# Two stacked graph attention layers: finishing work of the first entry spread over steps, the held row tile taken whole, first queries moved ahead

## The chip, the core and the metric

The kernel runs on one core of one Trainium2 chip. The metric is the device time in microseconds. Three runs of the kernel before gave 4408.67, 4412.6 and 4412.98, median 4412.6.

## The reference

`x` has 8 entries (batch) of 2048 rows and 256 columns; `adj` is a 2048 x 2048 integer mask. Cut to what matters:

```python
# layer 0: 8 heads of 32 columns
x_proj = einsum('bnd,hdf->bhnf', x, W)
e = leaky_relu(e_src[..., :, None] + e_dst[..., None, :], 0.2)
e = e + softplus(beta) * log(adj + 1e-6)          # where adj > 0
h = einsum('bhij,bhjf->bhif', softmax(e), x_proj)
x = layernorm(x + h.reshape(B, N, D) @ W_out.T)
# layer 1: one head
e = leaky_relu((x @ W1) @ (x @ W2).T, 0.2)        # where adj > 0
x = layernorm(x + relu(softmax(e) @ (x @ W3)))
```

## The kernel before

**Layer 0** (`class Gat`, one object per entry). The softmax over a row splits into products: the numerator for key row j and query row i is the larger of two factors times the mask, so that no exponential of a full matrix is needed. `step` does one unit of it: one of four head pairs (`hp`) and one of 16 tiles of key rows (`jt`), 64 units per entry. For each of the two heads VectorE makes `s` (L375) from the query factors `c`, a per-row scalar of `re`, and the mask tile `mt`. TensorE then multiplies `s` with the scaled values `v` into `val` and with `re` into `den`, the denominators (L410, both by `products`). For some units of later entries (`SUMMED`) the denominators are first added up by VectorE into `d` (L386), and TensorE sums `d` once at the end of the head pair.

When a head pair is done, `finish` copies `val` to `ht` and `den` to `dn`, turns the denominators into reciprocals (`rc`, L431), writes them to `rec_d` in DRAM, and, on every second head pair, loads them back spread over partitions (`rb`, L446) and multiplies each half of `ht` with them (L452). It is a generator: each `yield` is a place where it can be left and taken up later. Entries from 1 on put it into the list `later`, from which every `step` takes it one piece further; entry 0 runs it to its end at once (L401 to L403). For entry 0 `rb` lies in the two buffers of the tag `d`, which also take every second mask tile when `deep` is set (L201).

`factors` and `scale` prepare an entry: maxima and exponentials of the row scores (L280 to L288), and four multiplications of `v` (L294), each of four row tiles. `store` writes `v` and `re` to DRAM, and `load` brings `v` back in four pieces.

**Layer 1** (`class Dot`, one object per entry). `queries` makes `h1` for four row tiles (L530), `scores` the scores `e` of one row tile against all 2048 rows (L540) and their exponentials `p`, and `step` transposes `p` (`pt`, L563, copied to `pts`) and multiplies it with the values `h3` into `acc` (L579). It keeps one row tile ahead: while tile it is multiplied, the scores of it + 1 are made. `fill(0)`, `fill(1)` and `fill(2)` are places within `step` where units of the next entry's layer 0 are put. `output` (L479 to L492) makes `y`, adds the input tile `xg` and normalises it, four row tiles at a time; `turn` transposes it to `x1t` (L504) and makes `h3` (L510), eight pieces and a start.

**Order.** First layer 0 of entry 0 runs, and beside it the projections of the other seven entries (`others`, L270) and the weights. Then the loop at L669 interleaves layer 1 of entry b - 1 with layer 0 of entry b. TensorE's instructions are issued in the order of the program throughout (L88), those of the load queue on SyncE from L667 on. All other engines get an order from the scheduler when the kernel is built, and each engine then runs its own list in that order. Tiles of one tag share its buffers: a new tile waits until the last reader of an older one is done.

At each change of entry the last two row tiles of layer 1 are held back, and the first units of the next entry are put between their parts: tile 14 takes two units in `fill(1)` and two in `fill(2)`, tile 15 two in `fill(1)` together with the first piece of `output` (L694 to L699). Then come four groups of `output` with `turn` two groups behind, two units after each (L701 to L708), and then the new `Dot` with its queries and first scores.

Of the kernel before, what the change touches and what calls it, by code (L numbers as in the profile page):

```python
# [27 lines left out]
def kernel(  # L28
# [28 lines left out]
    H, _, DH = w_proj.shape  # L57
    NT = N // P
# [175 lines left out]
    class Gat:  # L234


        def __init__(self, b):
            self.b = b
            self.units = ((hp, jt) for hp in range(NP) for jt in range(NT))
            self.ms, self.mts = [], []  # L240
            self.later = gats[b - 1].later if b > 1 else []

        def begin(self, kept):

# [103 lines left out]
        def step(self, count=1):  # L348

            for _ in range(count):  # L350
                hp, jt = next(self.units)
                for work in list(self.later):
                    if next(work, self) is self:
                        self.later.remove(work)
                if self.b > 0 and hp == NP - 1 and jt == 0 and self.b + 1 < B:
                    gats[self.b + 1].load_factors()
                if jt == 0:
                    if self.b > 0:
                        self.cs = [self.cs_ahead.pop(0) for _ in range(HP)]
                    else:  # L360
                        self.cs = [self.query_rows(hp * HP + a) for a in range(HP)]
                    self.val = pacc.tile([P, HALF], F32, tag="val", name="val")
                    self.den = pacc.tile([P, HALF], F32, tag="den", name="den")
                first = self.b == 0 and hp == 0
                if first:
                    self.more_mt(jt + 2, jt > 0)
                if self.b > 0:
                    mt = self.mts.pop(0)
                else:
                    mt = self.mts[jt] if first else load_mt(jt, True)  # L370
                s = []
                for a in range(HP):
                    h = hp * HP + a
                    sa = wide_tile("s", "s", 4)
                    nc.vector.scalar_tensor_tensor(sa, self.cs[a], self.re[:, 0, jt, h:h + 1], mt, ALU.max, ALU.mult)  # L375
                    s.append(sa)
                    if self.b > 0 and jt == NT - 1:
                        self.cs_ahead += [c for c in [next(self.c_loads, None)] if c]
                if self.b > 0 and len(self.mts) < (4 if not SUMMED[self.b][hp] and jt < NT - 4 else 2):
                    self.mts += [t for t in [next(self.mt_loads, None)] if t]  # L380
                v, e = self.v, self.re[:, 1]
                heads = [hp * HP + a for a in range(HP)]
                chain = SUMMED[self.b][hp]
                if jt - 1 in chain[1:]:
                    for d, sa, h in zip(self.sums, self.last, heads):
                        nc.vector.scalar_tensor_tensor(d, sa, e[:, jt - 1, h:h + 1], d, ALU.mult, ALU.add)  # L386
                self.last = s
                self.products(self.val, [v[:, jt, ts(h, DH)] for h in heads], s, jt == 0, jt == NT - 1)
                if jt in chain[:1]:
                    self.sums = [wide_tile("d", "d", 2) for _ in heads]  # L390
                    for d, sa, h in zip(self.sums, s, heads):
                        nc.scalar.activation(d, sa, AF.Copy, scale=e[:, jt, h:h + 1])  # L392
                if jt not in chain:
                    self.products(self.den, [e[:, jt, h:h + 1].to_broadcast([P, DH]) for h in heads], s, jt == 0,
                                  not chain and jt == NT - 1)
                if chain and jt == NT - 1:
                    self.products(self.den, [ones] * HP, self.sums, False, True)
                if jt == NT - 1:
                    work = self.finish(hp)
                    next(work)  # L400
                    if self.b == 0:  # L401
                        for _ in work:
                            pass  # L403
                    else:
                        self.later.append(work)

        def products(self, dst, weights, s, start, stop):
            for c in range(HALF // BK):
# [46 lines left out]
        def output(self):  # L455


            b = self.b
            xb = x[b].rearrange("(t p) d -> p t d", p=P)
            xs = []  # L460

            def load(g):
                xs.append(chunk.tile([P, IG, D], F32, tag="ht", name="xg", bufs=3))
                nc.sync.dma_start(xs[g], xb[:, ts(g, IG), :])

            load(0)
            load(1)
            yield
            for g in range(NB):
                if 0 < g < NB - 1:  # L470
                    load(g + 1)
                st = small.tile([P, IG, nc.vector.BN_STATS_DIM], F32, name="st4", bufs=1)
                mv = small.tile([P, IG, nc.vector.BN_AGGR_DIM], F32, name="mv4", bufs=2)
                z = self.ht[:, ts(g, IG)].rearrange("p t k i -> p t (k i)")
                for k in range(0, IG, 2):
                    y = mm_tile("y").rearrange("p (t c) -> p t c", t=2)
                    for i in range(2):
                        for kc in range(KC):
                            nc.tensor.matmul(y[:, i, :], self.ht[:, g * IG + k + i, kc, :], wot[:, kc, :],  # L479
                                             start=(kc == 0), stop=(kc == KC - 1))  # L480
                    nc.vector.tensor_add(z[:, k:k + 2, :], y, xs[g][:, k:k + 2, :])
                    for i in range(k, k + 2):
                        nc.vector.bn_stats(st[:, i, :], z[:, i, :])
                        nc.vector.bn_aggr(mv[:, i, :], st[:, i, :])
                f = small.tile([P, 2, IG], F32, name="f4", bufs=2)
                nc.scalar.activation(f[:, 0, :], mv[:, :, 1], AF.Ln, bias=eps_ln)
                nc.scalar.activation(f[:, 0, :], f[:, 0, :], AF.Exp, scale=-0.5)
                nc.vector.scalar_tensor_tensor(f[:, 1, :], mv[:, :, 0], -1.0, f[:, 0, :], ALU.mult, ALU.mult)
                for k in range(IG):
                    nc.scalar.activation(z[:, k, :], z[:, k, :], AF.Identity, bias=f[:, 1, k:k + 1],  # L490
                                         scale=f[:, 0, k:k + 1])
                nc.scalar.dma_start(x1_d[b].rearrange("(t p) d -> p t d", p=P)[:, ts(g, IG), :], z)  # L492
                yield
# [22 lines left out]
    class Dot:  # L516


        def __init__(self, gat):
            self.b, self.x1t, self.h3 = gat.b, gat.x1t, gat.h3  # L520
            self.at = 0
            self.queries(0)
            self.scores(0)

        def queries(self, g):
            self.h1 = h1 = chunk.tile([P, KC, BK], F32, tag="ht", name="h1", bufs=3)
# [82 lines left out]
    def others():  # L609
# [1 line left out]

        order = gats[2:-2] + gats[1:2] + gats[-2:]
        groups = [(gat, g) for gat in order for g in range(NB)]
        xgs, xts = [], []

        def load(n):
            if n < len(groups):
# [11 lines left out]
        for n, (gat, g) in enumerate(groups):  # L629
            if g == 0:  # L630
                if gat is order[-1]:

                    for _ in range(IG):
                        yield
                gat.begin("h3" if n // NB % 2 or gat is order[-1] else "v")
            for k in range(IG):
                gat.row(g * IG + k, xts[n])
                if k == 1:
                    turn(n + 1)
                if g == NB - 1 and k == IG - 1:  # L640
                    gat.factors()
                    for i in range(NB):
                        gat.scale(i)
                    if gat.b > 1:
                        gat.store()
                if g == 0 and k == IG - 1 and n > 0:
                    groups[n - 1][0].queries()
                yield
        order[-1].queries()
        yield  # L650

# [17 lines left out]
    for b in range(1, B + 1):  # L669
# [11 lines left out]
        rows, turns = gat.output(), gat.turn()  # L681
        if dot is None:
            layer_0(4)
            next(rows)
            next(projections)
        else:

            dot.step(lambda k: layer_0((0, 2, 2)[k]))
            if not fresh:
                for work in gat.later:  # L690
                    for _ in work:
                        pass

            def fill(k):  # L694
                if k == 1:
                    layer_0(2)
                    next(rows)

            dot.step(fill)  # L699

        for g in range(NB + 2):  # L701
            if g < NB:
                next(rows)
            if g > 1:
                next(turns)
                next(turns)
            if g < NB + 1:
                layer_0(2)  # L708
        dot = Dot(gat)
        dot.step(lambda k: layer_0((2, 0, 2)[k]))  # L710
        count = NP * NT - (18 if b == 1 else 20)
        for i in range(NT - 3):
            n = (i + 1) * count // (NT - 3) - i * count // (NT - 3)
            dot.step(lambda k: layer_0((0, n - 2, 2)[k]))
# [31 lines left out]
```

## Time and profile before

| what | us | share |
|---|---|---|
| span of the profiled run | 4410.4 | |
| TensorE, matmuls | 4248.7 | 96% |
| VectorE | 3603.8 | 82% |
| ScalarE | 1663.4 | 38% |

By stage (busy time within a window, in us):

| window | what runs | TensorE | VectorE | DMA share |
|---|---|---|---|---|
| 0 to 160 | set-up, first head pair of entry 0 | 127.5 | 124.9 | 0.86 |
| 160 to 520 | rest of entry 0, projections | 326.1 | 291.7 | 0.73 |
| 596 to 1115 | layer 1 of entry 0, layer 0 of entry 1 | 499.1 | 436.8 | 0.62 |
| 1115 to 1626 | the same, one entry on | 499.8 | 449.9 | 0.53 |
| 4091 to 4410 | layer 1 of the last entry alone | 305.2 | 71.6 | 0.15 |

A row of the timeline has the start, the busy time, the engine, the line, the operation, the tiles, and in brackets the idle time before it and who ended that. A row of the waits has the engine and line that waited, what it waited for, the total in us, how often, and the longest. A row of the windows has, for each engine in turn, busy time and count, then the granted TensorE clock as a share of full speed, the DMA share and GB/s.

### The profile page before, as it was taken

Reading aid. Unit: us, or ns where it says so; the run is one execution under the profiler, and the core shown is the slowest. Engines: PE = TensorE matmul, PEld = TensorE weight load, DVE = VectorE, ACT = ScalarE, POOL = GpSimd, SP = SyncE. Lnnn points to the kernel's source line nnn. Section 1 sums busy time; section 2 is a strip of 40 time slices with the busy share of each in tenths; the row PEclk is TensorE's granted clock in tenths of the full one; section 3 lists DMA queues with packets and bytes.
Section 4 is the critical chain, followed back from the end, with each engine's and each line's share of the span. In section 5 each row is a group of like instructions: output and inputs, shape, how many; then the busy total and the mean of one; then the engine's idle time right before and its main releaser. Section 6 shows DMA issues by size and latency. Waiting matters only on the chain.

```text
span 4410.4 us, 59810 instructions
## 1 busy us (share of the span) xinstructions
PE 4248.7 (96%) x25072; PEld 2215.7 (50%) x25072; DVE 3603.8 (82%) x2606; ACT 1663.4 (38%) x3019; POOL 9.5 (0%) x14
## 2 busy tenths in 40 slices
PE   7989899998999999999999999999999999999999
PEld 4444354444555545554455544554455545555666
DVE  7878878898799988999789988999799997998222
ACT  7522143332333333433343333333333324333455
POOL 0000000000000000000000000000000000000000
PEclk9999999999999999999999999999999999999999
DMA  8867755656455564546555464555544465543211
GB/s 260 303 247 256 259 194 211 229 199 227 174 186 191 202 216 147 193 182 212 194 181 196 158 234 167 193 191 207 194 172 172 183 229 185 184 174 143 78 48 41
DMA packets 253166, 839.10 MB, mean 190 GB/s; under 512 B 32224, under 2 KB 150752, under 8 KB 178400
## 3 DMA queue, kind: packets, MB, share of 16 engines
q1 hardware_dynamic: 217568, 801.71, 51.2%
q10 hardware_dynamic: 35328, 33.56, 2.2%
q8 instruction: 196, 3.21, 0.3%
q14 instruction: 74, 0.61, 0.0%
HBM read 761.53 MB, written 73.14 MB: 189 GB/s over the span
## 4 chain that ended last, share of the span: by engine, by line
PE 50%; DVE 21%; issue 7%; DMA 7%; ACT 3%; SPq 1%; DVEq 0%; ACTq 0%
DVE s L375 14%; PE e L540 13%; PE acc L579 12%; PE val L410 10%; PE den L410 7%; DMA mt<-mt_d 4%; PE pt L563 3%; DVE d L386 3%; DMA rb<-rec_d 2%; PE h3p L510 2%; PE h1p L530 1%; PE y L479 1%; DVE p L545 1%; ACT d L392 1%; ACT p L548 1%
## 5 line engine op out<-in xcount | busy, mean ns | idle before, releaser
L375 DVE SCALAR_TENSOR_TENSOR s<-c,re,mt 128x2048 f32<-128x2048 f32 x1024 | 2354.2, 2342 | 218.6 <-PE den L410 141.0
L410 PE MATMUL val<-s,v 128*32 128x512 f32 x8192 | 1044.3, 605 | 90.7 <-DVE s L375 90.5
L579 PE MATMUL acc<-h,pts 128*128 128x256 f32 x4096 | 953.8, 380 | 12.1 <-ACT pts L565 12.1
L540 PE MATMUL e<-x1t,h 128*128 128x512 f32 x2048 | 905.2, 594 | 8.0 <-ACT h L532 8.0
L579 PEld LDWEIGHTS acc<-h,pts 128*128 128x128 f32 x4096 | 747.5, 190 | 107.4 <-ACT pts L565 22.1
L410 PE MATMUL den<-s,re 128*32 128x512 f32 x5648 | 706.1, 594 | 0.0
L386 DVE SCALAR_TENSOR_TENSOR d<-s,re,d 128x2048 f32<-128x2048 f32 x264 | 615.3, 2345 | 0.0
L540 PEld LDWEIGHTS e<-x1t,h 128*128 128x128 f32 x2048 | 379.4, 190 | 460.3 <-issue 415.8
L410 PEld LDWEIGHTS val<-s,v 128*32 128x32 f32 x8192 | 245.1, 110 | 723.0 <-issue 510.5
L565 ACT COPY pts<-pt 128x512 f32<-128x512 f32 x512 | 297.1, 583 | 762.6 <-PE pt L563 747.5
L545 DVE CUSTOM_DVE_ANT_0 p<-p,pen 128x2048 f32<-128x2048 f32 x128 | 292.7, 2286 | 243.8 <-ACT p L542 243.4
L542 ACT ACTIVATE p<-e 128x512 f32<-128x512 f32 x512 | 304.3, 595 | 466.3 <-PE e L540 459.5
L410 PEld LDWEIGHTS den<-s,re 128*32 128x32 f32 x5648 | 192.7, 110 | 426.0 <-issue 420.0
L563 PEld LDWEIGHTS pt<-ident,p 128*128 128x128 f32 x2048 | 239.0, 141 | 228.8 <-issue 182.7
L548 ACT ACTIVATE p<-p,neg 128x2048 f32<-128x2048 f32 x128 | 256.8, 2006 | 218.1 <-DVE neg L545 218.1
L563 PE MATMUL pt<-ident,p 128*128 128x128 f32 x2048 | 319.9, 279 | 5.1 <-ACT p L548 5.1
L585 DVE TENSOR_TENSOR z<-z,x1r 128x256 f32<-128x256 f32 x128 | 54.0, 422 | 182.7 <-ACT z L584 181.3
L584 ACT ACTIVATE z<-acc,rec 128x256 f32<-128x256 f32 x128 | 60.8, 475 | 373.3 <-PE acc L579 289.9
L510 PE MATMUL h3p<-w3s,x1t 128*128 128x256 f32 x512 | 124.7, 388 | 13.5 <-ACT x1t L505 13.0
L270 PE MATMUL proj<-wp,xt 128*128 128x272 f32 (+1 forms) x512 | 130.9, 401 | 3.2 <-ACT v L272 1.8
L272 ACT COPY v<-proj 128x256 f32<-128x256 f32 x128 | 47.0, 376 | 211.4 <-PE proj L270 197.5
L479 PE MATMUL y<-wot,ht 128*128 128x256 f32 x512 | 117.6, 383 | 0.0
(89 smaller groups left out, 1926.0 us busy)
## 6 DMA issues: line engine op xcount, KB each, us to landing
mt<-mt_d SPq DMA_DIRECT2D x496, 1024.0 KB
c<-c_d SPq DMA_DIRECT2D x64, 1024.0 KB
pen<-pen_d SPq DMA_DIRECT2D x112, 512.0 KB
xg<-in_x_dram SPq DMA_DIRECT2D x60, 512.0 KB
adj_t<-in_adj_dram SPq DMA_DIRECT2D x16, 1024.0 KB
mt_d<-mt SPq DMA_DIRECT2D x16, 1024.0 KB
rb<-rec_d SPq DMA_DIRECT2D x128, 128.0 KB
x_d<-ht ACTq DMA_DIRECT2D x32, 512.0 KB
```

The lines of the kernel that those rows point to most:

```text
L375: nc.vector.scalar_tensor_tensor(sa, self.cs[a], self.re[:, 0, jt, h:h + 1], mt, ALU.max, ALU.mult)
L386: nc.vector.scalar_tensor_tensor(d, sa, e[:, jt - 1, h:h + 1], d, ALU.mult, ALU.add)
L410: nc.tensor.matmul(dst[ts(q, DH), ts(c, BK)], weights[q % 2], s[q % 2][:, ds(q // 2 * HALF + c * BK, BK)], start=start, stop=stop)
L479: nc.tensor.matmul(y[:, i, :], self.ht[:, g * IG + k + i, kc, :], wot[:, kc, :], start=(kc == 0), stop=(kc == KC - 1))
L510: nc.tensor.matmul(t[:, ts(i, D)], x1t[:, kc, ts(2 * (j - 1) + i, P)], w3s[:, kc, :], start=(kc == 0), stop=(kc == KC - 1))
L540: nc.tensor.matmul(t, self.h1[:, kc, ts(it % IG, P)], self.x1t[:, kc, ts(c, BK)], start=(kc == 0), stop=(kc == KC - 1))
L542: nc.scalar.activation(p[:, ts(c, BK)], t, AF.Prelu, alpha=ALPHA)
L545: nc.vector.tensor_tensor_reduce(p, p, pen, -1.0, FMAX, ALU.add, ALU.min, neg)
L548: nc.scalar.activation(p, p, AF.Exp, bias=neg, scale=-1.0, accum_out=den)
L563: nc.tensor.transpose(t[:, ts(k, P)], p[:, ts(g * IG + k, P)], ident)
L565: nc.scalar.copy(pt, t)
L579: nc.tensor.matmul(acc, now[:, ts(k, P)], self.h3[:, j, :], start=(j == 0), stop=(j == NT - 1))
```

## The change

It has four parts. Entry 0's `finish` is no longer run to its end at once but put into `later` as for the other entries; the last one is carried on by entry 1's steps. The scalings of an entry's `v` and its `store` are spread over the next row tiles of the projections rather than done in a row. The last held row tile of layer 1 (15) is done in one piece, with two units of the next entry before it (in tile 14's `fill(2)`) and two behind it. And the new `Dot` makes its first queries before the last piece of `turn`, which makes the last values `h3`; its first scores come behind as before. `output` loads one input tile ahead from the start rather than two at once. The first entry takes 20 units ahead of layer 1's main loop, as the others do, rather than 18. The purpose is to keep TensorE supplied at these joints.

```diff
@@ class Gat
-            self.later = gats[b - 1].later if b > 1 else []
+            self.later = gats[b - 1].later if b > 0 else []
...
                     work = self.finish(hp)
                     next(work)
-                    if self.b == 0:
-                        for _ in work:
-                            pass
-                    else:
-                        self.later.append(work)
+                    self.later.append(work)
@@ output
             load(0)
-            load(1)
             yield
             for g in range(NB):
-                if 0 < g < NB - 1:
+                if g < NB - 1:
                     load(g + 1)
@@ Dot.__init__
             self.queries(0)
-            self.scores(0)
@@ others
                 if g == NB - 1 and k == IG - 1:
                     gat.factors()
-                    for i in range(NB):
-                        gat.scale(i)
+                    gat.scale(0)
+                    later = [lambda gat=gat, i=i: gat.scale(i) for i in range(1, NB)]
                     if gat.b > 1:
-                        gat.store()
+                        later.append(gat.store)
@@ main loop
             layer_0(4)
+            next(projections)
             next(rows)
-            next(projections)
         else:
             dot.step(lambda k: layer_0((0, 2, 2)[k]))
...
-            def fill(k):
-                if k == 1:
-                    layer_0(2)
-                    next(rows)
-
-            dot.step(fill)
+            next(rows)
+            dot.step()
+        layer_0(2)
 
         for g in range(NB + 2):
             if g < NB:
                 next(rows)
             if g > 1:
                 next(turns)
+                if g == NB + 1:
+                    dot = Dot(gat)
                 next(turns)
             if g < NB + 1:
                 layer_0(2)
-        dot = Dot(gat)
+        dot.scores(0)
         dot.step(lambda k: layer_0((2, 0, 2)[k]))
-        count = NP * NT - (18 if b == 1 else 20)
+        count = NP * NT - 20
```

In `others` one entry of the list `later` is taken after each row tile.

## The prediction

> **What bounds the kernel now.** I read the busy shares and the costliest groups first, then busy time by stage, then TensorE's gaps in the timeline, then what VectorE waits for at those gaps.
>
> ```profile
> PE 4248.7 (96%) x25072; PEld 2215.7 (50%) x25072; DVE 3603.8 (82%) x2606; ACT 1663.4 (38%) x3019; POOL 9.5 (0%) x14
> ...
> L375 DVE SCALAR_TENSOR_TENSOR s<-c,re,mt 128x2048 f32<-128x2048 f32 x1024 | 2354.2, 2342 | 218.6 <-PE den L410 141.0
> ```
>
> TensorE is the wall: 161.7 of 4410.4 us are not busy, so all that a reordering can win lies in there. VectorE mostly waits for TensorE (141.0 us before L375). The windows of the middle entries confirm it (1115 to 1626 us: TensorE 499.8 of 511). The gaps sit at the joints:
>
> ```profile
> DVE ht L452 <- DMA rb<-rec_d: 7.0, 1, 7.0
> DVE s L375 <- DMA mt<-mt_d: 3.7, 1, 3.7
> ...
> 303.32 1.92 PE L410 MATMUL val<-s,v 128*32 128x512 f32 x2 [11.07 <-DVE s L375]
> 507.97 1.92 PE L410 MATMUL val<-s,v 128*32 128x512 f32 x2 [12.15 <-DVE s L375]
> ...
> 1556.52 1.92 PE L410 MATMUL val<-s,v 128*32 128x512 f32 x2 [3.75 <-DVE s L375]
> 1580.33 1.06 PE L410 MATMUL val<-s,v 128*32 128x512 f32 x8 [1.68 <-DVE s L375]
> 1644.31 1.99 PE L510 MATMUL h3p<-w3s,x1t 128*128 128x256 f32 x8 [1.34 <-ACT x1t L505]
> 1650.63 0.70 PE L540 MATMUL e<-x1t,h 128*128 128x512 f32 x1 [0.90 <-ACT h L532]
> ...
> 304.00:310.00 6.00, 5.65 (x26) 1.09 (x27) 6.00 (x3) 0.00 (x0) 0.00 (x0) 0.53 0.98 397
> 1540.00:1606.00 66.00, 59.09 (x362) 30.98 (x364) 59.55 (x61) 14.96 (x35) 0.00 (x0) 0.95 0.63 209
> ```
>
> The bracket is TensorE's idle time before the row and who ended it. The two waits of VectorE (280 to 312 us) are those behind the 11.07: entry 0's division waits for its denominators, and the next mask tile could only load after it. In the windows the columns are TensorE, weight load, VectorE, ScalarE, GpSimd, clock: after a long gap the clock is 0.53 for 6 us, and in 1540 to 1606 both engines have nearly the same busy time (59.1 and 59.6 of 66).
>
> **The skill.** "TensorE: Matmul & The Clock Gate", Part 1, says the array falls to half clock after some 3.4 us idle. The trace agrees: 0.53 above, and 0.50 in 1556 to 1562 after the 3.75. So a gap of 4 us or more costs some 3 us on top (6 us at half speed), unless VectorE is late anyway. "Perfetto Trace Analysis", Identifying the Most-Contended Engine, warns that TensorE's busy share overstates it, while VectorE's occupancy is fair; hence I price joints by VectorE's list of work. "DMA: Bandwidth & Descriptors", Bandwidth, gives 435 GB/s as the ceiling; windows here show up to 423 (508 to 514 us).
>
> **The parts.** A unit is one `step` of layer 0: two L375 (2 x 2.3 = 4.6 us) on VectorE, `val` and `den` on TensorE (1.7 us each net, 3.65 with the tail). Units are counted from 0 at each head pair. The changed program's instruction order, as built, tells what stands behind what.
>
> 1. *Entry 0, second head pair done (gap at 303).* The division no longer blocks: unit 1's L375 follow at once (they end near 291.8 instead of 305.5), units 2 and 3 end near 296.8 and 302.1 (unit 3's tile takes the slot of unit 1's and is asked for at 291.8; loads here land in 4.8 to 6 us). TensorE finishes unit 3 at 306.0 instead of 321.1, about 11.07 plus the clock's 3 and a little waiting. But a wait comes instead: the order now has the factors (L280) and four L294 of a later entry *before* unit 5, where the kernel before had them after it. L280 waits for that entry's last projection, which TensorE reaches at 309.8 (unit 3 + 4.8 of projections, as from 321.1 to 325.9): 310.5 + 2.1 (L280 to L294, as at 326.85 to 328.97) + 4.6 + second multiply 1.2 + 4.6 = 323.0 for unit 5, while TensorE ended unit 4 at 314.4. New gap 8.6. Then projections, unit 6: it ends at 333.6 (336 with a cold clock) instead of 341.3. Taken: **-7** (bounds -2 and -14).
>
> 2. *Entry 0 to 1 (gap at 508).* VectorE idles for 3.78 (mask tile) plus some 5 us from 490 on. Spread out it does unit 1 at 490.0 to 494.6, factors and one L294 to 498.2, units 2, 3 to 507.4, three L294 to 510.9, unit 4 to 515.5, unit 5 with the first multiply to 521.3, unit 6 525.9, unit 7 530.5, layer norm of the first group with second multiply to 536.2, unit 8 540.8, unit 9 (adds of the next group between its halves, 3.2) 548.6. A unit takes VectorE 4.6 and TensorE 3.65, so TensorE starves: 3.3 + 4.4 + 2.1 + 1.1 + 4.1 = 15.0 us idle, against 12.15 + 1.22 + 0.55 and some 2.5 of half clock = 16.4 before. The `y` work that filled it now comes two units later. Behind the mask tile that waits for the first multiply stand `v_d`, `c_d`, the second pair of `rb` loads and unit 8's tile: 5 MB at about 423 GB/s is 12 us from 519, landing near 531, in time for 536. Taken: **-1** (bounds -7 and +5).
>
> 3. *Held row tile undivided (six joints, entries 1 to 6 to their followers).* TensorE does `acc` before units 4 and 5, filling the gap of 3.75. But VectorE's list from unit 4 (1546.19) to unit 7 is the same: four L375 pairs 18.4, four L386 9.4, two multiplies 2.4, row tile and first group some 4: about 34, and it runs with 0.8 us idle. Unit 7 is ready near 1580.2 in both (before: 1580.28). The gap moves behind `y`: TensorE is free at 1564.8 and gets unit 6 at 1572.3. Unit 9 ends near 1596 in both, perhaps a little later by the clock. Taken: 5 x +0.5; at the first such joint, where the mask tiles come late (a wait of 3.97 before unit 4), +2 by the same sum. Together 4.5, taken as **+4** (bounds +12 and -39, rival B).
>
> 4. *First queries ahead of the last values.* `h1p` (3.60 us) needs only the first 512 columns of `x1t`, ready long before. It fills the wait for the last `x1t` copy, and the last `h3p` (1.9) hides the copies of `h1`. Gaps removed at six joints: 1.33 or 1.34 each, 8.0 in all, and before `e` 1.05, 0.90, 0.76, 0.57 and 0.72 at five of them, 4.0 in all. Taken **-12**; the last joint has no such gap (`h3p` runs on into `h1p` there). The wait for a third PSUM buffer is hidden: each tile's copy is done one group earlier.
>
> 5. *Scaling spread, and one prefetch of `xg`.* In most places the order still has four L294 in a row, so the 4.18 gap at 444 stays. Near 144 one L294 falls behind unit 6's pair: **-1**. The `xg` loads cost nothing: they come earlier or at the same place, ahead of mask tiles that land before use. Entry 1 starts layer 1 two units further: same work, shared 44 to 13 instead of 46; 0, within 3.
>
> Sum: -7 - 1 + 4 - 12 - 1 = -17, 4412.6 to **4396**.
>
> **The rivals.**
> A, the two long gaps of entry 0 vanish whole: -14 and -15.5 instead of -7 and -1, 4374. For it: VectorE is only 291.7 of 360 us busy from 160 to 520 and could catch up. Against: the order of L280 above.
> B, the held tile wins its gap: 3.75 + 0.35 + some 3 of clock at six joints is 41 beside my 4: about 4351. For it: the wait is in the trace. Against: VectorE's full list until unit 7.
> C, waits take the place of those removed: the slots that `rb` shares with the mask tiles starve VectorE (part 1 at 0, part 2 at +8), and each held tile loses 2.5 as TensorE idles 7.5 us and comes back at half clock (+15): 0 + 8 + 15 - 12 = +11, about 4424, slower.
>
> **Numbers.** My forecast 0.68, spread about 8 us either way from parts 1, 2, 3; A 0.12, B 0.08, C 0.12. Within 0.2% means 4403.8 to 4421.4. About a sixth of the forecast's weight lies above 4403.8, so faster is 0.76, same 0.14, slower 0.10. The range leaves out B and most of C: 4372 to 4413.
>
> **What would show it.** Right: no gap at 303, a new one of 8 to 9 us some 15 to 20 us later before a `val`, ended by L375; smaller gaps adding to about 15 between 495 and 550; in each later joint no gap before `acc` but 4 to 8 us behind the first `y` group; none before the last `h3p`. Wrong: steps of later entries shorter than 508 us (B), or VectorE waiting for `mt` or `rb` for over 5 us after the first multiply (C).

## The result, and the profile after

The changed kernel takes 4390.02 us (median of 4 runs, 4388.77 to 4394.88) beside 4412.79 for the kernel before on the same chip: ratio 0.9952, 95% interval 0.9935 to 0.9970. That is about 21 us less (13 to 29 by the interval), where the prediction said 17 less (4396) and gave 4372 to 4413 as its range. The profiled run of the changed kernel is its slowest (4394.88, span 4393.1), so its trace shows only 17.3 us of the gain. Everywhere below, times on different chips are compared by their ratios to the kernel before, timed beside them.

Lines have moved up: L406 are now the products (before L410), L427 the reciprocal, L448 the multiplication with `rb`, L474 `y`, L505 `h3p`, L524 `h1p`, L534 `e`, L573 `acc` (in the runs below lines shift by a few again). TensorE's groups that wait at the joints, of the kernel before:

```profile
L410 PE MATMUL val<-s,v 128*32 128x512 f32 x8192 | 1044.3, 605 | 90.7 <-DVE s L375 90.5
L579 PE MATMUL acc<-h,pts 128*128 128x256 f32 x4096 | 953.8, 380 | 12.1 <-ACT pts L565 12.1
L540 PE MATMUL e<-x1t,h 128*128 128x512 f32 x2048 | 905.2, 594 | 8.0 <-ACT h L532 8.0
L510 PE MATMUL h3p<-w3s,x1t 128*128 128x256 f32 x512 | 124.7, 388 | 13.5 <-ACT x1t L505 13.0
```

The busy shares of the changed kernel, VectorE's `s`, and the same four groups:

```profile
PE 4245.8 (97%) x25072; PEld 2220.1 (51%) x25072; DVE 3603.9 (82%) x2606; ACT 1661.8 (38%) x3019; POOL 9.5 (0%) x14
...
L375 DVE SCALAR_TENSOR_TENSOR s<-c,re,mt 128x2048 f32<-128x2048 f32 x1024 | 2353.6, 2342 | 225.4 <-PE den L406 150.8
L406 PE MATMUL val<-s,v 128*32 128x512 f32 x8192 | 1041.2, 606 | 84.9 <-DVE s L375 84.9
L573 PE MATMUL acc<-h,pts 128*128 128x256 f32 x4096 | 954.4, 381 | 16.7 <-ACT pts L559 16.6
L534 PE MATMUL e<-x1t,h 128*128 128x512 f32 x2048 | 904.5, 594 | 3.3 <-ACT h L526 3.2
...
L505 PE MATMUL h3p<-w3s,x1t 128*128 128x256 f32 x512 | 122.7, 383 | 4.8 <-ACT x1t L500 4.3
```

The work is the same on every engine: same counts, busy times within 3 us. What has changed is above all TensorE's idle time: 161.7 us before, 147.3 now, that is 14.4 of the 17.3. The `h3p` group had 13.5 us idle ahead of it and the `e` group 8.0; now they have 4.8 and 3.3. TensorE's wait for `s` has hardly shrunk, from 90.7 to 84.9, and that before `acc` has grown by 4.6. So the waits at the joints of layer 0 have mostly moved. The timeline shows where to, in TensorE's rows and, for the first, in VectorE's:

```profile
313.27 0.37 DVE L280 TENSOR_REDUCE top<-both 128x8 f32<-128x128 f32 x1 [2.37 <-ACT both L274]
...
315.40 4.63 DVE L294 TENSOR_TENSOR v<-v,re 128x1024 f32<-128x1024 f32 x4 [0.63 <-ACT re L288]
319.95 1.22 DVE L448 TENSOR_TENSOR ht<-ht,rb 128x1024 f32<-128x1024 f32 x1
321.14 9.14 DVE L375 SCALAR_TENSOR_TENSOR s<-c,re,mt 128x2048 f32<-128x2048 f32 x4
...
323.55 1.91 PE L406 MATMUL val<-s,v 128*32 128x512 f32 x2 [6.31 <-DVE s L375]
...
1559.71 1.04 PE L406 MATMUL val<-s,v 128*32 128x512 f32 x2 [1.92 <-DVE s L375]
...
1563.35 2.78 PE L406 MATMUL val<-s,v 128*32 128x512 f32 x11 [2.60 <-DVE s L375]
...
1572.16 2.70 PE L406 MATMUL val<-s,v 128*32 128x512 f32 x11 [2.37 <-DVE s L375]
```

The gap of 11.07 at 303 is gone, and one of 6.31 stands 20 us later. Ahead of unit 5's `s` VectorE has the factors of a later entry (L280, for which it waits 2.37), four scalings (4.63) and the second half of the division (1.22). In a later joint the gap of 3.75 before `acc` is gone, and three gaps (6.9 us together) stand in the units behind the first `y`.

To place the gain I lay the two traces on each other. The start of the first addition of `z` in layer 1, which VectorE does at the same place of the program in both:

| entry of layer 1 | before | after | difference |
|---|---|---|---|
| 1 | 1169.4 | 1161.7 | -7.7 |
| 2 | 1680.3 | 1671.0 | -9.2 |
| 3 | 2189.8 | 2178.7 | -11.2 |
| 4 | 2700.2 | 2687.0 | -13.2 |
| 5 | 3211.8 | 3196.6 | -15.2 |
| 6 | 3722.0 | 3706.3 | -15.7 |
| 7 | 4167.8 | 4150.6 | -17.3 |

The set-up of this run was 2.2 us slower than that of the run before (unit 0 of the third head pair begins at 282.4 instead of 280.2), and 4.0 us ahead by 389: about -6.2 in entry 0. From there to the first `z` of entry 1 another 3.7 come, and then some 2 us from most entries (0.5 to 2.0).

### The profile page after: what moved, and what is told of

Read it like the earlier page. It is cut to its first block, busy times and chain, and to the rows that moved or that the text cites. A ratio compares the mean times of both kernels' runs of the same rounds, so it can differ in the third digit from the quotient of the medians.

```text
span 4393.1 us, 59809 instructions
## 1 busy us (share of the span) xinstructions
PE 4245.8 (97%) x25072; PEld 2220.1 (51%) x25072; DVE 3603.9 (82%) x2606; ACT 1661.8 (38%) x3019; POOL 9.5 (0%) x14
## 4 chain that ended last, share of the span: by engine, by line
PE 56%; DVE 20%; issue 8%; DMA 7%; ACT 2%; SPq 1%; POOL 0%; DVEq 0%; ACTq 0%; POOLq 0%
DVE s L375 14%; PE e L534 14%; PE val L406 12%; PE acc L573 12%; PE den L406 9%; PE pt L557 3%; DMA mt<-mt_d 3%; DVE d L386 3%; PE h3p L505 2%; PE h1p L524 2%; DMA rb<-rec_d 1%; DVE p L539 1%; DMA xg<-in_x_dram 1%; PE y L474 1%; PE proj L270 1%
## 5 line engine op out<-in xcount | busy, mean ns | idle before, releaser
L375 DVE SCALAR_TENSOR_TENSOR s<-c,re,mt 128x2048 f32<-128x2048 f32 x1024 | 2353.6, 2342 | 225.4 <-PE den L406 150.8
L406 PE MATMUL val<-s,v 128*32 128x512 f32 x8192 | 1041.2, 606 | 84.9 <-DVE s L375 84.9
L573 PE MATMUL acc<-h,pts 128*128 128x256 f32 x4096 | 954.4, 381 | 16.7 <-ACT pts L559 16.6
L534 PE MATMUL e<-x1t,h 128*128 128x512 f32 x2048 | 904.5, 594 | 3.3 <-ACT h L526 3.2
L573 PEld LDWEIGHTS acc<-h,pts 128*128 128x128 f32 x4096 | 747.9, 190 | 113.0 <-ACT pts L559 28.4
L406 PE MATMUL den<-s,re 128*32 128x512 f32 x5648 | 727.1, 601 | 0.0
L534 PEld LDWEIGHTS e<-x1t,h 128*128 128x128 f32 x2048 | 380.2, 190 | 450.1 <-issue 415.6
L406 PEld LDWEIGHTS val<-s,v 128*32 128x32 f32 x8192 | 245.6, 110 | 707.1 <-issue 517.1
L406 PEld LDWEIGHTS den<-s,re 128*32 128x32 f32 x5648 | 198.0, 112 | 436.1 <-issue 429.7
L505 PE MATMUL h3p<-w3s,x1t 128*128 128x256 f32 x512 | 122.7, 383 | 4.8 <-ACT x1t L500 4.3
L474 PE MATMUL y<-wot,ht 128*128 128x256 f32 x512 | 118.3, 385 | 0.0
```

What stands on the lines that cost most here:

```text
L406: nc.tensor.matmul(dst[ts(q, DH), ts(c, BK)], weights[q % 2], s[q % 2][:, ds(q // 2 * HALF + c * BK, BK)], start=start, stop=stop)
L505: nc.tensor.matmul(t[:, ts(i, D)], x1t[:, kc, ts(2 * (j - 1) + i, P)], w3s[:, kc, :], start=(kc == 0), stop=(kc == KC - 1))
L534: nc.tensor.matmul(t, self.h1[:, kc, ts(it % IG, P)], self.x1t[:, kc, ts(c, BK)], start=(kc == 0), stop=(kc == KC - 1))
L573: nc.tensor.matmul(acc, now[:, ts(k, P)], self.h3[:, j, :], start=(j == 0), stop=(j == NT - 1))
```

## The experiments

Each was timed in turn with the kernel before on the same chip (medians of before 4414.14, 4414.56 and 4414.68). The times together; `b_` names are built on the kernel before, `a_` names on the changed one:

| run | median us | ratio to before | interval |
|---|---|---|---|
| changed kernel | 4390.02 | 0.9952 | 0.9935 to 0.9970 |
| b_queries | 4401.72 | 0.9967 | 0.9954 to 0.9979 |
| b_held | 4414.91 | 0.9999 | 0.9990 to 1.0007 |
| b_entry0 | 4419.22 | 1.0010 | 1.0001 to 1.0018 |
| b_entry0_20 | 4408.90 | 0.9987 | 0.9980 to 0.9994 |
| a_divided | 4392.88 | 0.9952 | 0.9939 to 0.9964 |
| a_factors | 4391.27 | 0.9943 | 0.9930 to 0.9955 |
| a_factors23 | 4384.42 | 0.9931 | 0.9918 to 0.9943 |
| a_late_sums | 4370.82 | 0.9900 | 0.9887 to 0.9914 |
| a_late_divided | 4367.13 | 0.9891 | 0.9877 to 0.9904 |
| a_best | 4360.16 | 0.9877 | 0.9862 to 0.9892 |

**b_queries: the queries alone.**

```diff
@@ Dot.__init__
             self.queries(0)
-            self.scores(0)
@@ main loop
                 next(turns)
+                if g == NB + 1:
+                    dot = Dot(gat)
                 next(turns)
...
-        dot = Dot(gat)
+        dot.scores(0)
```

> The kernel before with one part alone: the first queries of layer 1 ahead of the last piece of turn. Theory (a wait of TensorE filled with ready work): the two waits, before the last h3p (1.33 each) and before the first e (0.57 to 1.05), go at six joints; in the trace of the changed kernel its lead grows by 2.1 to 2.7 us across each of these stretches, a little more than the two waits. So -12 to -16 us, about 4398. Rival (the time is given back): the first scores wait for another copy instead, or the gain in the changed kernel is owed to the held tile that ends earlier: within 4 us of before.

Measured: 0.9967, which is -14.6 us (-20.3 to -9.3). The theory holds. The timeline of the second joint, first of the kernel before and then of b_queries (TensorE rows):

```profile
1641.08 1.89 PE L510 MATMUL h3p<-w3s,x1t 128*128 128x256 f32 x8
1644.31 1.99 PE L510 MATMUL h3p<-w3s,x1t 128*128 128x256 f32 x8 [1.34 <-ACT x1t L505]
1646.14 3.60 PE L530 MATMUL h1p<-x1t,w 128*128 128x512 f32 x8
1650.63 7.13 PE L540 MATMUL e<-x1t,h 128*128 128x512 f32 x16 [0.90 <-ACT h L532]
```

```profile
1640.51 1.89 PE L510 MATMUL h3p<-w3s,x1t 128*128 128x256 f32 x8
1642.24 3.60 PE L529 MATMUL h1p<-x1t,w 128*128 128x512 f32 x8
1645.68 1.89 PE L510 MATMUL h3p<-w3s,x1t 128*128 128x256 f32 x8
1647.40 7.03 PE L539 MATMUL e<-x1t,h 128*128 128x512 f32 x16
```

From the first row to the first `e` it is 9.55 us before (1641.08 to 1650.63) and 6.89 after (1640.51 to 1647.40): 2.66 less, although the two waits shown are 2.24 together. The other 0.42 is what a stop costs beside its idle time: rows without a stop begin 0.16 before the row ahead of them has ended (1646.14 against 1644.31 + 1.99), and a row behind a stop takes 0.10 longer (1.99 for 1.89, 7.13 for 7.03). Between these two rows lie 0.16 twice and 0.10 once, which is the 0.42. (The profile models where a matmul ends, so I go by the starts.) The same stretch in all six joints was 8.89 to 9.70 us long before and is 6.89 to 6.92 now: 14.8 us less together, as the times say, of which the brackets are 12.3.

**b_held: the held row tile alone** (six joints from entry 1 on).

```diff
-            def fill(k):
-                if k == 1:
-                    layer_0(2)
-                    next(rows)
-            dot.step(fill)
+            next(rows)
+            dot.step()
+            layer_0(2)
```

> The kernel before with one part alone: at the six joints from entry 1 on, the last held row tile in one piece, with its two units behind it. Theory (VectorE's list sets the end of the joint, TensorE's gap only moves behind the first y): no gap before acc, gaps of 6 to 8 us in the units behind y, +4 us, between 0 and +8, about 4417. Rival B of the prediction (the gap is TensorE's own and goes): -41, about 4372.

Measured: 0.9999, -0.4 us (-4.4 to +3.1). Rival B is out: 41 us are not there. The gap has only moved, as its timeline shows in the joint where the 3.75 was:

```profile
1578.10 1.91 PE L410 MATMUL val<-s,v 128*32 128x512 f32 x2 [5.57 <-DVE s L375]
1581.08 2.78 PE L410 MATMUL val<-s,v 128*32 128x512 f32 x11 [1.07 <-DVE s L375]
```

5.57 and 1.07 stand for the 3.75, 0.35 twice and 1.68 of before (6.1). The half clock comes once in both; it lasts longer here (0.50 from 1575.8 to 1586.1, in before from 1555.5 to 1562.4), and yet this joint takes no longer: VectorE, busy for 24.3 of the 26 us from 1566 to 1592, most likely sets the pace. From the `z` of row tile 13 to the first `z` of the next entry, the first such joint takes 2.5 us longer in this trace than in that of before, and the other five take 0.4 to 1.5 us less each.

**a_divided: the same part undone in the changed kernel** (the diff above backwards, at the same joints).

> The changed kernel with the last held row tile divided again (two units before acc, as before), all else of the change kept. The prediction's step 3 (the gap only moves, +4 for the undivided tile): about 4 us less than the changed kernel, 4386. Reading of b_held (nothing, within its interval): 4390, ratio 0.994 to 0.9955. Rival B (the undivided tile wins its gap): 4400 or more.

Measured: 0.9952, the changed kernel's own ratio. Here too the undivided tile is worth nothing that these runs can tell from zero, so the step's +4 is not confirmed either. Over the six joints the two traces differ by 0.1 us.

**b_entry0: entry 0's finish in pieces, alone.**

```diff
-            self.later = gats[b - 1].later if b > 1 else []
+            self.later = gats[b - 1].later if b > 0 else []
...
-                    if self.b == 0:
-                        for _ in work:
-                            pass
-                    else:
-                        self.later.append(work)
+                    self.later.append(work)
```

> The kernel before with one part alone: entry 0's finish left in pieces to the next units, and its last one to entry 1. Theory: the gap of 11.07 at 303 goes and one of 6 to 9 comes behind unit 4, where a later entry's factors and four scalings stand before unit 5; entry 0 to 1 changes by less than 3. Together -6 to -9 us, about 4405. Rival A (both gaps of entry 0 vanish whole): -30, about 4383. Second rival (the gain seen in the profile is scatter of the set-up): within 3 us of before.

With the old layout of 18 units the first `y` group of entry 0 is computed ahead of the last division, so these rows enter layer 1 undivided; only the time is of use. Measured: 1.0010, which is 4.4 us more (0.4 to 7.9). Up to 480 its trace does what was expected: `s` of the third head pair, 1.1 us behind the trace of before at its start, is 5.7 ahead at its end, so -6.8, with a gap of 6.36 before unit 5's `val`. Then it loses more than that. The timeline, in the joint of entry 0 and 1:

```profile
539.15 5.03 PE L475 MATMUL y<-wot,ht 128*128 128x256 f32 x14 [18.31 <-DVE ht L448]
```

The division comes in pieces of one per unit, and the first multiplication comes with the sixth unit of entry 1. Four units are not enough for it: the second group of `y` has to wait for the multiplication, which itself waits 8.3 us until the first group, computed in the same half of `ht`, is stored. So the two further units that the change gives entry 1 are no detail beside this part but what makes it possible.

**b_entry0_20: with these two units.** To the diff of b_entry0 this is added:

```diff
             layer_0(4)
-            next(rows)
             next(projections)
+            next(rows)
+            layer_0(2)
...
-        count = NP * NT - (18 if b == 1 else 20)
+        count = NP * NT - 20
```

> As b_entry0, with the two further units that the change gives entry 1 ahead of layer 1 (20 instead of 18; the change needs them, since in b_entry0 TensorE stood 18.31 us before the first y, which waits for entry 0's last division). Theory: 6 to 7 us less up to 480, as b_entry0's trace shows, and about nothing from 480 to 620: 4407, 0.998 to 0.9985. Rival A of the prediction (both gaps of entry 0 vanish whole): 4383. Rival: the joint of entry 0 and 1 gives it back, 4414.

Measured: 0.9987, -5.7 us (-8.8 to -2.6). In its trace the third head pair gains 6.3 (from 3.2 behind to 3.1 ahead), and some 2 us of it are given back between there and the first `z` of entry 1. Nothing like the stop of 18.31 is left in the joint. Rival A (-30) is out, and so is a joint that gives it all back.

**a_factors: the factors of later entries put off.** In the changed kernel, so that VectorE has them behind unit 8 and not before unit 5.

```diff
-                        later.pop(0)()
+                        for work in later[:3]:
+                            work()
+                        later = later[3:]
...
-                    gat.factors()
-                    gat.scale(0)
-                    later = [lambda gat=gat, i=i: gat.scale(i) for i in range(1, NB)]
+                    later = [lambda: None] * 4 + [gat.factors] + [lambda gat=gat, i=i: gat.scale(i) for i in range(NB)]
...
-                if g == 0 and k == IG - 1 and n > 0:
-                    groups[n - 1][0].queries()
+                if g == 1 and k == IG - 1 and n > NB:
+                    groups[n - 2][0].queries()
```

> The changed kernel, with a later entry's factors and scalings put five row tiles of the projections further on (and its est four), so that on VectorE they stand behind unit 8 of the third head pair and not before unit 5. Theory (unit 5 waits because these stand before it, 2.37 for the last projection and 6.7 of work): the gap of 6.31 at 323 and the 2.9 before unit 6's L375 go, some 5 to 9 us less than the changed kernel, about 4383. Rival (unit 5 waits for its mask tile, which loads only after the first multiply): the same gap stays with a transfer as its cause, 4390.

Measured: 0.9943, which is 4 us less than the changed kernel by the ratios, but the two intervals overlap for most of their width: no gain that can be told from zero. But the gap of 6.31 is gone; of it, 1.01 and 1.22 are left at unit 5's `val`. So the order of the factors was its cause. Part of what this wins was lost ahead of it. VectorE's row of the timeline shows where:

```profile
192.04 4.62 DVE L375 SCALAR_TENSOR_TENSOR s<-c,re,mt 128x2048 f32<-128x2048 f32 x2 [12.21 <-DMA mt<-mt_d]
```

The factors of the first entries moved too, the units before them ran earlier, and the mask tile for the second head pair's first unit, read back from DRAM, then kept VectorE waiting 12.21 us; in the changed kernel the same pair begins at 183.6. The second head pair begins 10.7 us behind the trace of before and ends 3.2 behind it; the fourth begins 10.9 ahead of it, where the changed kernel is 4.0 ahead. Why that tile lands so late was not tried, nor why the times show less than the 6.9 that the trace has here.

**a_factors23: only the third and fourth entries in the row put off.** The diff is that of a_factors under `if n // NB in (2, 3)`; the others stay as in the changed kernel.

> As a_factors, but only the third and the fourth of the entries in the row have their factors put off; the first ones stay where the changed kernel has them, since in a_factors VectorE waited 12.21 us at 192 for a mask tile and lost 8 us that the third head pair then gave back. Theory: no gap at 323 and none of 6 at 194, so about 6 to 10 us less than the changed kernel, about 4383. Rival (the loss at 192 belongs to the freed time and comes back elsewhere): 4390.

Measured: 0.9931, 9 us less than the changed kernel by the ratios, 5.6 by the medians; the two intervals just overlap (0.9918 to 0.9943 and 0.9935 to 0.9970). Its timeline where the 6.31 was:

```profile
304.44 1.05 PE L406 MATMUL val<-s,v 128*32 128x512 f32 x2 [1.47 <-DVE s L375]
306.70 2.75 PE L406 MATMUL val<-s,v 128*32 128x512 f32 x11 [1.22 <-DVE s L375]
```

2.7 us are left in place of 6.31; its third head pair ends 6.0 us ahead of the changed kernel's, and its run too.

**a_late_sums: VectorE relieved at the joints.** The sums of denominators keep their number; only their units change. With them goes some of TensorE's work: a unit in this list has no `den` of its own (some 1.7 us), so units 2, 4 and 5 now have it, and 9, 11 and 13 do not.

```diff
-    SUMMED += [[(2, 4, 5)] + [(1, 3, 5, 7, 9, 11, 13)] * (NP - 1)] * (B - 2)
+    SUMMED += [[(9, 11, 13)] + [(1, 3, 5, 7, 9, 11, 13)] * (NP - 1)] * (B - 2)
```

> The changed kernel, with the sums of denominators of each entry's first head pair (entries 2 to 7) at units 9, 11, 13 instead of 2, 4, 5: as many for VectorE and TensorE, but out of the joint. Theory (VectorE's list from unit 4 to 7 sets the joint): the list is 9.4 us shorter at each of six joints, the gaps behind y (1.9, 2.6, 2.4 in the steady ones, 5.75 in the first) go or come below 1 us each: -25 to -45, about 4355. Rival (something else, a mask tile, the y adds or the clock, sets it): within 8 us of the changed kernel, 4390.

Measured: 0.9900, 4370.82: about 23 us less than the changed kernel by the ratios (0.9952 and 0.9900), and the intervals do not meet. The rival is out, the theory's size was a little too high (25 to 45). The timeline of the joint at 1560, all that is left behind `y`:

```profile
1560.24 1.49 PE L406 MATMUL val<-s,v 128*32 128x512 f32 x11 [0.45 <-DVE s L375]
...
1572.48 1.92 PE L406 MATMUL val<-s,v 128*32 128x512 f32 x14 [0.55 <-DVE s L375]
```

And the windows from 1540 to 1566 of the changed kernel and of a_late_sums (columns as in the prediction: TensorE, weight load, VectorE, ScalarE, GpSimd, clock, DMA share, GB/s):

```profile
1540.00:1566.00 26.00, 21.24 (x126) 12.49 (x122) 26.00 (x24) 4.15 (x10) 0.00 (x0) 0.92 0.54 167
```

```profile
1540.00:1566.00 26.00, 25.55 (x178) 12.79 (x177) 21.14 (x24) 5.07 (x13) 0.00 (x0) 1.00 0.57 203
```

VectorE was busy for all 26 us, TensorE for 21.24; with the sums gone VectorE has 21.14, TensorE 25.55, at full clock. (In the second trace `acc` begins 5.8 us sooner, so the same window lies a little further on in the program.) The run changes both lists of the joint at once, VectorE's by 9.4 us less and TensorE's by some 5 us more; which of the two closed the gaps, it does not separate. What the size missed: where the sums now stand, two gaps of 1.34 and 1.22 have come (at 1613.92 and 1616.19), and 0.89 before an `h3p`.

**a_late_divided: the same with the held tile divided.**

> As a_late_sums, with the last held row tile divided as in the kernel before. Theory (where the held tile stands does not matter, VectorE's list does): within 5 us of a_late_sums. Rival (with room on VectorE the undivided tile wins its gap, rival B in a milder form): a_late_sums is better by 10 to 25 us.

Measured: 0.9891 against 0.9900: the divided tile is no worse even where VectorE has room. The rival is out. In this trace the clock stays full from 545 to 4098, and TensorE's busy time is 4235.6 us, 13 less than in the kernel before.

**a_best: a_late_divided with a_factors23.**

> a_late_divided together with a_factors23: entry 0's finish in pieces, the queries ahead, the held tile divided, sums of denominators late, two factors put off. If the gains lie at different places they add: 4367 less 6 to 8, about 4360. Rival: what factors23 wins is lost in entry 1, which VectorE then holds up: 4367.

Measured: 4360.16, ratio 0.9877: 54 us less than the kernel before by its ratio, 33 less than the changed kernel. It is 6 us below a_late_divided by the ratios, as hoped, though the two intervals overlap, and it leaves the held tile as it was before the change.

## Why the prediction was right, step by step

The forecast hit the side and the size, and most of the places. Its terms were off by up to some 4 us each, and in the sum these errors partly cancel: that it came so near to the measured 21 is in part luck. By its steps:

1. *Entry 0, -7.* Right. The gap at 303 went, one came 20 us later (said: 15 to 20) ended by L375, for the reason named: the factors and four scalings before unit 5, as a_factors shows by taking them away. It is 6.31 and not 8.6: the sum let `val` wait for both L375 of unit 5, but it starts behind the first, 2.3 earlier. In the trace this stretch gave 6.2, in b_entry0_20 6.3.
2. *Entry 0 to 1, -1.* About right. The 12.15 did go to pieces, but those between 495 and 550 add up to 10.5 us, not 15.0. From the start of entry 1 to the end of its first stretch with layer 1 (some 1030 us) the changed kernel wins 2.0 us, while b_entry0_20 gives 1.4 back; the -1 lies between. By the times b_entry0_20 has -5.7 for steps 1, 2 and the two units together, where the prediction had -8, which its interval does not exclude. That these units cost "0" hid that they are needed: b_entry0 without them was slower than before.
3. *Held row tile, +4.* Right in the mechanism: the gap goes from `acc` to the units behind `y`, 6.9 us in the joint at 1560 (said: 4 to 8). The size was off: by the times b_held says -0.4 and a_divided 0. The +2 for the first such joint fits (2.5 in b_held's trace); the term that failed is the five times +0.5 for a later end, where b_held's trace has 0.4 to 1.5 us less each.
4. *Queries, -12.* Right in the mechanism; the times give -14.6, with an interval that has room for -12. The traces say that it was too small: the term took the brackets alone (12.3 in the trace), and the stretch became 14.8 shorter over the six joints. The missing 2.5 is what two stops cost beside their brackets, 0.42 in the joint shown.
5. *Scaling spread and one prefetch of `xg`, -1.* Not run alone. The gap of 4.18 at 444 stayed, as was said (4.17 at 440.26). The loads of `xg` were said to cost nothing, but in the joint of entries 0 and 1 VectorE now waits for one, which it does neither in the kernel before nor in b_entry0_20:

```profile
528.73 1.29 DVE L476 TENSOR_TENSOR ht<-y,xg 128x512 f32<-128x512 f32 x2 [3.32 <-DMA xg<-in_x_dram]
```

What this cost, if anything, was not separated.

The parts add up: -14.6 - 0.4 - 5.7 = -20.7 for the three that ran alone, beside -21 for the whole. Against the -16 that the prediction had for the same parts, step 3 makes 4.4 and step 4 2.6 of difference, and steps 1 and 2 go the other way by 2.3; of the three, only step 3's +4 lies outside the interval of its part (up to 3.1). The rivals fell each by a run: A by b_entry0_20, B by b_held and, with VectorE relieved, by a_late_divided. (The sign named for B, entries shorter than 508 us, shows once, 507.7 from entry 2 to 3; B itself asks for some 7 us less in each.) Of C, one piece was real and only just avoided: a division that comes late stops TensorE, as b_entry0 shows.

One sentence at the start was too narrow: that all a reordering can win lies in TensorE's 161.7 idle us. In a_late_divided TensorE's idle time fell by 38 us and its busy time by 13, with the same instructions and less half clock.

Steps 2 and 3 were priced by VectorE's list of work. "Perfetto Trace Analysis", Identifying the Most-Contended Engine, calls the busy share a fair measure of how near VectorE is to its limit, and not a good one for TensorE's matmuls. The trace agrees: from 1540 to 1566 VectorE is busy for 26 us out of 26, and it is the one that ends TensorE's gaps.

## What to carry to other kernels

When a gap of the busiest engine is ended by another engine that has no idle time there, reordering the first engine's own work only moves the gap (-0.4 us in b_held). The balance of the two lists in that stretch has to change, and work that may be done anywhere (here 9.4 us of sums) should be done where that engine has room: that gave 23 us. A wait filled with work that is ready long before was worth its bracket and a little more (14.8 us for 12.3). When a long step is spread over units, count the units until its result is needed, and look again at what now stands in line before the next unit.

## What was not expected of the hardware

The clock fell after shorter gaps than the 3.75 and 11.07 of before. In the changed kernel it fell at 1562.06, within the second of two gaps, 1.92 and 2.60 with 1.04 of work between them, and at 1572.30, just behind the single gap of 2.37. In the kernel before, the 1.68 at 1580 left it at 1.00. "TensorE: Matmul & The Clock Gate", Part 1, gives some 3.4 us of idle time; here 2.37 was enough, 1.68 was not.

The length of a gap is not what decides in these traces. In each of the twelve traces kept (before, after and the ten runs), all changes of the clock lie whole multiples of 3.41 us apart. So I cut each trace into steps of 3.41 us, at the times where the clock can change, and look at TensorE's busy time in each step. First two pairs of neighbouring steps of the changed kernel, then two neighbours of the kernel before (the first number behind the comma is TensorE's busy time, the third from the end the clock):

```profile
1558.65:1562.06 3.41, 1.04 (x2) 0.14 (x2) 3.41 (x7) 0.00 (x0) 0.00 (x0) 1.00 0.11 38
1562.06:1565.47 3.41, 2.12 (x12) 0.59 (x16) 3.41 (x5) 0.00 (x0) 0.00 (x0) 0.50 0.34 55
1568.88:1572.29 3.41, 1.04 (x12) 0.13 (x8) 2.53 (x2) 1.97 (x4) 0.00 (x0) 1.00 0.14 47
1572.30:1575.71 3.41, 3.41 (x20) 0.87 (x20) 3.41 (x2) 0.00 (x0) 0.00 (x0) 0.50 1.05 303
...
1576.02:1579.43 3.41, 2.63 (x22) 0.50 (x14) 3.41 (x5) 0.00 (x0) 0.00 (x0) 1.00 0.11 38
1579.43:1582.84 3.41, 2.51 (x24) 0.80 (x27) 3.41 (x5) 0.57 (x3) 0.00 (x0) 1.00 0.47 120
```

A step with 1.04 us of work is followed by half clock, twice. The gap of 1.68 lies across the border of two steps, each of which has over 2.5 us of work left, and the clock stays. Over all steps of the twelve traces the clock fell after every one that was busy for less than 0.41 of its time and after none with more than 0.47. It came back after every one with more than 0.83 and after none with less than 0.77. So the price of a gap depends on where it lies between these borders, and the half clock lasts a whole number of steps. The prediction's 3 us for a gap of 4 us or more is one case of this.
